# A four-layer graph network on one core: spreading the loop products over the first edge groups, and moving three weight loads

## The chip, the cores and the metric

The kernel runs on one core of one Trainium2 chip. The metric is the device time of one execution in microseconds (us), as the median of several runs. Engines are called as in the profile: PE (TensorE matmuls), PEld (TensorE weight loads), DVE (VectorE), ACT (ScalarE), POOL (GpSimd), SP (SyncE, which here only issues transfers).

## The reference

1024 nodes with 512 features, 17408 edges sorted by target node, all in float32. Four graph layers follow each other, each on the normalized, rectified features, each added back to `x`. The change lies in the last one, called block 3 here, which runs the following layer twice (8 relations, 4 bases):

```python
hb = jnp.einsum('nd,bdo->bno', h, basis)
coef = comp[etypes]
m = sum(coef[:, b, None] * hb[b][src] for b in range(4))
m = m * norm[:, None]
agg = jax.ops.segment_sum(m, dst, num_segments=n)
out = agg + bias + h @ loop_w
if apply_relu: out = relu(out)
```

The first layer (l = 0) has the relu, the second (l = 1) has not. `h @ loop_w` is the "loop product", `loop_w` the "loop weights".

## The kernel before, in words

The kernel first sums the edges' source rows per target and basis, and multiplies by the basis afterwards. Nodes come in 8 blocks of 128 (`n`), features in 4 chunks of 128 (`c`), edges in 68 groups of 256 (`g`; two tiles of 128, `k`). Only the arm `fast` runs here.

For each layer `l` of block 3, the loop at L1142 and following does this for each group `g`:

1. Two gathers on POOL (`gathered`, L1122 to L1129, `gather`, L289) fetch the 256 source rows of the *next* group from the table `htabs[l]` in HBM into tiles `m`. Eleven tiles exist for them (5 `m`, 4 `h`, 2 `hq`); a gather waits until the group that used its tile eleven gathers earlier is done.
2. DVE builds the weighted one-hot `wo` of the next group (L1135).
3. PE multiplies `m` and `wo` into `ps` (L1149, 16 matmul records per group).
4. At some groups (the table at L1151) PE also does the loop product of one node block `n`: `loop0(n)` for l = 0 (L1048, `dense`, matmuls on L251), and for l = 1 a transposition `turned5(n + 1)` (L241) and `loop1(n)` (L251, added by DVE at L1111; POOL adds the bias at L1112). The products of blocks 0 to 2 come ahead of group 0, those of 3 to 7 are in the table.
5. From group 11 on, when the sums of node block 0 are complete (`settled`), PE does two steps per group of the basis products (`products`, L1094, `po`), 16 steps per node block. Those left over come behind the last group.
6. DVE adds `ps` into `sums` (L1168).

A finished node block goes through `ready` (L1076 to L1087). For l = 0 it is added, rectified and stored by SP's queue to the table `htabs[1]` (L1082); the first gather of layer 1 needs all eight of these stores. For l = 1 it is stored to the output (L1087).

Weights: a pool of six half-tiles (512 KB each, tag `w`) holds the loop weights and bases 0 and 1 of a layer; basis 2 lies in `w_l0`, and basis 3 in the one tile `w4` (1 MB, L1104). All of these loads go by SP's queue. The loop weights of layer 1 are loaded in layer 0 behind group 8 (L1161, `loop_weights`: two halves and the bias row). Bases 0 to 2 of layer 1 and then basis 3 are loaded when the last products of layer 0 have released their tiles.

The order on each engine is not that of the text: a planner issues what it reckons ready first. `tc.issue_after(i)` queues what is traced in its body behind instruction `i` on `i`'s engine, without a wait for its end.

Of the kernel before, what the change touches and what calls it, by code (L numbers as in the profile page):

```python
# [21 lines left out]
P = 128  # L22
# [10 lines left out]
NBAS = 4  # L33
# [3 lines left out]
G = 2  # L37
# [12 lines left out]
def gnn_stack(ctx, tc, a, out, xtab, htabs, hidtab):  # L50
# [6 lines left out]
    nc = tc.nc  # L57
# [23 lines left out]
    src_i = const.tile([P, ET], I32, name="src_i")  # L81
# [6 lines left out]
    def half_w(name):  # L88
        return wpool.tile([P, 2, D], F32, tag="w", name=name, bufs=6)

    def load_half(w, ap, h):
        nc.sync.dma_start(w, ap.rearrange("(h c p) o -> h p c o", h=2, p=P)[h])
        return w
# [193 lines left out]
        return nc.vector.tensor_sub(lo, rest, mid).ins  # L287

    def gather(g, table, idx, t):  # L289
        nc.gpsimd.indirect_dma_start(  # L290
            out=g, out_offset=None, in_=table,
            in_offset=bass.IndirectOffsetOnAxis(ap=idx[:, t : t + 1], axis=0))

# [93 lines left out]
    def stack(fast):  # L387
# [529 lines left out]
        with tc.tile_pool(name=f"l2{fast}", bufs=1) as l2:  # L917
# [107 lines left out]
            def loop_weights(l):  # L1025
                return load_w(a[f"L3_gnn_loop{l}"], f"loop{l}{fast}"), bias_row(f"L3_gnn_bias{l}", f"l3_{l}{fast}")

            def bases(l):

                ws = [load_w(a[f"L3_gnn_basis{l}"][b], f"basis{l}_{b}{fast}") for b in range(2)]  # L1030
                return ws + [[load_half(w_l0[h], a[f"L3_gnn_basis{l}"][2], h) for h in range(2)]]
# [33 lines left out]
        with tc.tile_pool(name=f"l3{fast}", bufs=1, reuse_waits="tile") as l3:  # L1065

            sums = l3.tile([P, KC, NBAS, N], F32, name="sums")
            if fast:
# [5 lines left out]
                    nc.scalar.activation(sums[:, 1, 2:4], nil.to_broadcast([P, 2 * N]).rearrange("p (b d) -> p b d", b=2), AF.Copy)  # L1074
                nc.gpsimd.memset(sums[:, 3], 0.0)

            def ready(l, n, po):

                if l == 0:
                    nc.vector.tensor_add(hb[:, n, :], hb[:, n, :], po)  # L1080
                    nc.scalar.activation(hb[:, n, :], hb[:, n, :], AF.Relu)  # L1081
                    nc.sync.dma_start(htabs[1][n * P : (n + 1) * P, :], hb[:, n, :])  # L1082
                    if fast:
                        nc.gpsimd.memset(sums.rearrange("p c b d -> p (c b) d")[:, :, n * P : (n + 1) * P], 0.0)
                else:
                    nc.vector.tensor_add(x[:, n, :], x[:, n, :], po)
                    nc.sync.dma_start(out[n * P : (n + 1) * P, :], x[:, n, :])  # L1087
# [12 lines left out]
            for l in range(2):  # L1100
                if l == 1:
                    w3 = [loops[1][0]] + bases(l)
                w = l3.tile([P, KC, D], F32, tag="w4", name=f"basis{l}_{NBAS - 1}{fast}")
                nc.sync.dma_start(w, a[f"L3_gnn_basis{l}"][NBAS - 1].rearrange("(c p) o -> p c o", p=P))  # L1104
                w3.append(w)
                with tc.tile_pool(name=f"l3e{l}{fast}", bufs=3 if fast else 1, reuse_waits="tile") as l3e:
                    def turned5(n):
                        hT3[n] = transposed(hb[:, n, :], f"l3_1_{n}")

                    def loop1(n):  # L1110
                        nc.vector.tensor_add(x[:, n, :], x[:, n, :], dense(hT3[n], w3[0], f"pl_1_{n}"))  # L1111
                        nc.gpsimd.tensor_add(x[:, n, :], x[:, n, :], loops[1][1])  # L1112

                    if l == 1:
                        turned5(0)
                        for n in range(3 if fast else NB):
                            if n + 1 < NB:
                                turned5(n + 1)
                            loop1(n)

                    homes = 5 * [(l3e, "m", 5)] + 4 * [(work, "h", 4)] + 2 * [(small, "hq", 2)]

                    def gathered(g):
                        m = []
                        for k in range(G):
                            pool, tag, bufs = homes[(g * G + k) % len(homes)]
                            m.append(pool.tile([P, D], F32, tag=tag, name=f"m_{l}_{g}_{k}", bufs=bufs))
                            gather(m[k], htabs[l], src_i, g * G + k)
                        return m  # L1129

                    if fast:
                        def weighted(g):
                            wo = l3e.tile([P, G, NBAS, W], F32, tag="wo", name=f"wo_{l}_{g}")
                            ts = slice(g * G, (g + 1) * G)
                            nc.vector.tensor_mul(wo, ohw[:, ts, :].unsqueeze(2).to_broadcast([P, G, NBAS, W]),  # L1135
                                                 cw[:, l, ts, :].unsqueeze(3).to_broadcast([P, G, NBAS, W]))
                            return wo

                        todo = (step for n in range(NB) for step in products(l, n, w3))
                        given = 0  # L1140
                        nxt = gathered(0), weighted(0)
                        for g in range(NG):  # L1142
                            m, wo = nxt
                            if g + 1 < NG:
                                nxt = gathered(g + 1), weighted(g + 1)
                            ps = bank(f"ps_{l}_{g}")
                            for c in range(KC):
                                for k in range(G):
                                    nc.tensor.matmul(ps[:, c * P : (c + 1) * P], m[k][:, c * P : (c + 1) * P],  # L1149
                                                     wo[:, k].rearrange("p b w -> p (b w)"), start=(k == 0), stop=(k == G - 1))  # L1150
                            n = {0: 3, 1: 4, 2: 5, 4: 6, 6: 7}.get(g)  # L1151
                            if n is not None:
                                if l == 0:
                                    loop0(n)
                                else:
                                    if n + 1 < NB:
                                        turned5(n + 1)
                                    loop1(n)
                            if l == 0 and g == 8:

                                loops[1] = loop_weights(1)  # L1161
                            done = sum(settled(n) <= g for n in range(NB - 1))
                            for _ in range(2):
                                if given < done * NBAS * KC:
                                    next(todo)
                                    given += 1
                            part = sums.rearrange("p c b d -> p (c b) d")[:, :, bass.ds(base(g), W)]
                            nc.vector.tensor_add(part, part, ps.rearrange("p (i w) -> p i w", w=W))  # L1168
                        for _ in todo:
                            pass  # L1170
                    else:
                        for g in range(NG):
                            m = gathered(g)
                            for b in range(NBAS):
                                for j in range(2):
                                    wo = l3e.tile([P, G, 512], F32, tag="wo", name=f"wo_{l}_{g}_{b}_{j}")
                                    for k in range(G):
                                        t = g * G + k
                                        nc.vector.tensor_scalar(wo[:, k, :], iota[:, j * 512 : (j + 1) * 512], dst_f[:, t : t + 1],
                                                                cw[:, l, t, b : b + 1], op0=ALU.is_equal, op1=ALU.mult)  # L1180
                                    for c in range(KC):
                                        ps = bank(f"ps_{l}_{g}_{b}_{j}_{c}")
                                        for k in range(G):
                                            nc.tensor.matmul(ps, m[k][:, c * P : (c + 1) * P], wo[:, k, :],
                                                             start=(k == 0), stop=(k == G - 1))
                                        part = sums[:, c, b, j * 512 : (j + 1) * 512]
                                        if g == 0:
                                            nc.vector.tensor_copy(part, ps)
                                        else:
                                            nc.vector.tensor_add(part, part, ps)  # L1190
                        for n in range(NB):
                            for _ in products(l, n, w3):
                                pass
                        if l == 0:
                            loops[1] = loop_weights(1)
# [65 lines left out]
```

## Time and profile before

| | |
|---|---|
| runs | 1237.68, 1236.44, 1232.68 us; median 1236.44 |
| profiled execution | 1221.29 us |
| its span, first to last instruction | 1219.5 us |
| PE busy in the span | 1195.6 us (98%) |
| POOL busy in the span | 580.5 us (48%) |
| mean granted PE clock | 0.994 |

The profiled execution is 15 us shorter than the median of the runs; nothing in the profile says why. Block 3 starts with the first loop product at 688.8 us of the span; layer 0's groups start at 699.9 us, its last products end at 951.9 us, layer 1's groups start at 963.1 us and its last matmuls at 1212 us. A time such as 963.1 us is always counted from the start of the span. Matmul durations in the rows overlap; what one group costs PE is read from the starts of neighbours: 1.78 us for the `ps` of one group, 3.43 us for a loop product, 0.43 us for a transposition, 1.72 us for two steps of basis products.

### The profile page before, as it was taken

What the parts mean: (1) busy time and instruction counts of PE and PEld (TensorE: products, weight loads), DVE (VectorE), ACT (ScalarE), POOL (GpSimd) and SP (SyncE); (2) the same over time, 40 slices, a digit from 0 to 9 for tenths busy, and PEclk for the clock granted to TensorE, in tenths of its full rate; (3) what the DMA queues carried; (4) which work ended last, traced back from release to release, by engine and by line L of the source; (5) the groups of instructions that cost most, each with busy time, mean ns of one, the idle gap of its engine ahead of it and who ended that gap; (6) DMA issues with size and microseconds to landing.
All of it is one profiled execution on the core that took longest, in us unless ns stands there. A gap on an engine that the chain in (4) does not pass through costs nothing.

```text
span 1219.5 us, 17420 instructions
## 1 busy us (share of the span) xinstructions
PE 1195.6 (98%) x6322; PEld 795.8 (65%) x6322; DVE 661.8 (54%) x1244; ACT 295.0 (24%) x693; POOL 580.5 (48%) x641
## 2 busy tenths in 40 slices
PE   7999999999999999999999999999999999999998
PEld 3445557767777778644444567777776577777774
DVE  5888647786777775776774433333332153333331
ACT  4435364434444443432332400000000000000000
POOL 2011346686666663443121266566661586555540
PEclk9999999989999999999999999999999999999999
DMA  3331045545544442002002366555552666556540
GB/s 114 124 125 36 22 155 165 151 139 153 151 139 139 139 130 85 21 22 65 1 9 92 101 193 206 160 164 157 165 163 65 199 170 194 162 162 170 157 129 17
DMA packets 55166, 149.77 MB, mean 123 GB/s; under 512 B 8796, under 2 KB 10272, under 8 KB 55008
## 3 DMA queue, kind: packets, MB, share of 16 engines
q0 software_dynamic: 33360, 109.34, 31.3%
q1 hardware_dynamic: 21424, 38.71, 9.6%
q8 instruction: 52, 0.85, 0.3%
q10 hardware_dynamic: 288, 0.52, 0.1%
q14 instruction: 42, 0.34, 0.1%
HBM read 135.70 MB, written 12.85 MB: 122 GB/s over the span
## 4 chain that ended last, share of the span: by engine, by line
PE 89%; DVE 4%; issue 2%; DMA 2%; ACT 1%; POOL 1%; DVEq 0%; SPq 0%; ACTq 0%; POOLq 0%
PE ps L1149 19%; PE po L1094 18%; PE pg L885 14%; PE pu L275 10%; PE pw L819 10%; PE p L955 7%; PE pl L251 4%; PE pm L453 2%; PE po L803 1%; PE pz L251 1%; PE pt_l L241 1%; PE pc L532 1%; DVE cnt L545 1%; PE pup L689 1%; DMA w_mlp<-in_L_gnn_W_mlp_dram 1%
## 5 line engine op out<-in xcount | busy, mean ns | idle before, releaser
L290 POOL DMA_INDIRECT m<-htab_dram,src_i x272 | 261.2, 960 | 165.6 <-PE ps L1149 116.9
L1149 PEld LDWEIGHTS ps<-wo,m 128*128 128x128 f32 x2176 | 261.6, 192 | 57.3 <-issue 56.0
L1149 PE MATMUL ps<-wo,m 128*128 128x128 f32 x2176 | 262.2, 275 | 0.7 <-DMA m<-htab_dram,src_i 0.7
L885 PEld LDWEIGHTS pg<-yo,msg 128*128 128x128 f32 x1632 | 194.6, 193 | 35.9 <-issue 17.8
L885 PE MATMUL pg<-yo,msg 128*128 128x32 f32 (+1 forms) x1632 | 189.8, 274 | 2.7 <-DVE msg L841 1.5
L1168 DVE TENSOR_TENSOR sums<-sums,ps 128x512 f32 x136 | 93.7, 689 | 156.7 <-PE po L1094 133.8
L836 ACT ACTIVATE dot<-s,ea 128x128 f32<-128x128 f32 x408 | 130.0, 390 | 165.7 <-DVE msg L841 107.5
L290 POOL DMA_INDIRECT s<-xtab_dram,src_i x136 | 132.8, 976 | 36.4 <-issue 24.5
L819 PE MATMUL pw<-w_mlp,hq 128*128 128x512 f32 x272 | 135.1, 620 | 0.0
L1135 DVE TENSOR_TENSOR wo<-ohw,cwTrue 128x256 f32<-128x256 f16 x136 | 65.9, 487 | 103.5 <-PE ps L1149 103.5
L859 POOL TENSOR_TENSOR yo<-ohw,ea 128x160 f32<-128x160 f16 x136 | 63.1, 486 | 66.6 <-PE pg L885 66.5
L275 PE MATMUL pu<-parts,cnt 128*128 128x512 bf16 x384 | 84.8, 379 | 0.0
L837 DVE TENSOR_TENSOR msg<-pw,s 128x512 f32<-128x512 f32 x68 | 47.0, 692 | 47.3 <-PE pw L819 35.6
L819 PEld LDWEIGHTS pw<-w_mlp,hq 128*128 128x128 f32 x272 | 47.2, 193 | 34.0 <-issue 34.0
L275 PEld LDWEIGHTS <-cnt 128*128 128x128 f16 x384 | 37.6, 98 | 44.9 <-issue 2.3
L838 DVE TENSOR_TENSOR msg<-s,pw 128x768 f32<-128x768 f32 x68 | 64.2, 944 | 0.0
L1094 PE MATMUL po<-basis_0True,sums 128*128 128x512 f32 x128 | 60.8, 600 | 0.4
L1094 PE MATMUL po<-basis_3True,sums 128*128 128x512 f32 x128 | 59.8, 594 | 0.8 <-DVE sums L1168 0.8
L1081 ACT ACTIVATE stage<-stage 128x512 f32<-128x512 f32 x8 | 5.0, 630 | 226.9 <-DVE stage L1080 226.9
L1094 PE MATMUL po<-w_l,sums 128*128 128x512 f32 x128 | 59.9, 593 | 0.0
L1094 PE MATMUL po<-basis_1True,sums 128*128 128x512 f32 x128 | 59.9, 593 | 0.0
L888 DVE TENSOR_TENSOR acc<-acc,pg 128x256 f32 x68 | 28.7, 422 | 46.7 <-PE pg L885 46.7
(208 smaller groups left out, 1355.2 us busy)
## 6 DMA issues: line engine op xcount, KB each, us to landing
hq<-hidtab_dram SPq DMA_DIRECT2D x17, 256.0 KB, 2.9
m<-htab_dram,src_i POOLq DMA_INDIRECT x272, 3.6
hidtab_dram<-hid POOLq DMA_DIRECT2D x9, 256.0 KB, 2.3
s<-xtab_dram,src_i POOLq DMA_INDIRECT x136, 3.6
xtab_dram<-up SPq DMA_DIRECT2D x8, 256.0 KB, 2.0
b_1True<-in_L_gnn_W_dram SPq DMA_DIRECT2D x4, 512.0 KB, 5.0
w_l<-in_L_gnn_basis_dram SPq DMA_DIRECT2D x4, 512.0 KB, 4.3
basis_0True<-in_L_gnn_basis_dram SPq DMA_DIRECT2D x4, 512.0 KB, 4.0
```

The lines of the kernel that those rows point to most:

```text
L275: nc.tensor.matmul(pu, m[:, s, d * P : (d + 1) * P], z[:, s, :], start=(s == 0 and j == 0), stop=(s == NB - 1 and j == len(zs) - 1))
L290: nc.gpsimd.indirect_dma_start(out=g, out_offset=None, in_=table, in_offset=bass.IndirectOffsetOnAxis(ap=idx[:, t : t + 1], axis=0))
L819: nc.tensor.matmul(pw[:, k, :], hq[q][:, (t % 4) * P : (t % 4 + 1) * P], w_mlp4[:, t // 4 % 2, :], start=True, stop=True)
L836: nc.scalar.activation(dot[:, k, m, :], s1[:, k, m, :], AF.Copy, scale=ea[:, g * G + k, 1 + m : 2 + m])
L838: nc.vector.tensor_mul(msg[:, :, 2:5, :], s1, w[:, :, 2:3, :].to_broadcast([P, G, 3, MUL]))
L859: nc.gpsimd.tensor_mul(yo[:, k], ohw[:, t, :].unsqueeze(1).to_broadcast([P, NY, W]), ea[:, t, :].unsqueeze(2).to_broadcast([P, NY, W]))
L885: nc.tensor.matmul(ps[:, b : b + n, :], lhsT, rhs, start=(k == 0), stop=(k == G - 1))
L955: nc.tensor.matmul(p, lhs[:, c, :], rhs[:, c, :], start=(c == 0), stop=(c == 1))
L1094: nc.tensor.matmul(po, sums[:, c, b, n * P : (n + 1) * P], chunk(w3[1 + b], c), start=(b == 0 and c == 0), stop=(b == NBAS - 1 and c == KC ...
L1135: nc.vector.tensor_mul(wo, ohw[:, ts, :].unsqueeze(2).to_broadcast([P, G, NBAS, W]), cw[:, l, ts, :].unsqueeze(3).to_broadcast([P, G, NBAS ...
L1149: nc.tensor.matmul(ps[:, c * P : (c + 1) * P], m[k][:, c * P : (c + 1) * P], wo[:, k].rearrange("p b w -> p (b w)"), start=(k == 0), stop= ...
L1168: nc.vector.tensor_add(part, part, ps.rearrange("p (i w) -> p i w", w=W))
```

## The change

It has three parts.

**The table of loop products.** Block 3 stays with loop products 3 to 7 between groups, but 4 to 7 are put behind groups 2, 4, 6 and 9, not 1, 2, 4 and 6.

**The loop weights of layer 1.** They are no longer loaded behind group 8 of layer 0 in one go but in two halves, behind groups 24 and 32, each queued on SP behind the last store that has been traced.

**Basis 3 of layer 1.** Its 1 MB load leaves SP's queue. POOL issues it at group 2 of layer 1, behind the gathers of group 3. For layer 0 it stays where it was.

```diff
     def gather(g, table, idx, t):
-        nc.gpsimd.indirect_dma_start(
+        return nc.gpsimd.indirect_dma_start(
...
+            def loop_halves(l):
+
+                w = [half_w(f"loop{l}_{h}{fast}") for h in range(2)]
+                for h in range(2):
+                    load_half(w[h], a[f"L3_gnn_loop{l}"], h)
+                    if h == 0:
+                        loops[l] = w, bias_row(f"L3_gnn_bias{l}", f"l3_{l}{fast}")
+                    yield
...
+            stored, sent = [], []
...
-                    nc.sync.dma_start(htabs[1][n * P : (n + 1) * P, :], hb[:, n, :])
+                    stored.append(nc.sync.dma_start(htabs[1][n * P : (n + 1) * P, :], hb[:, n, :]).ins)
...
-                nc.sync.dma_start(w, a[f"L3_gnn_basis{l}"][NBAS - 1].rearrange("(c p) o -> p c o", p=P))
+                rows = a[f"L3_gnn_basis{l}"][NBAS - 1].rearrange("(c p) o -> p c o", p=P)
+                if l == 0 or not fast:
+                    nc.sync.dma_start(w, rows)
...
-                            gather(m[k], htabs[l], src_i, g * G + k)
+                            sent.append(gather(m[k], htabs[l], src_i, g * G + k).ins)
...
-                            n = {0: 3, 1: 4, 2: 5, 4: 6, 6: 7}.get(g)
+                            n = {0: 3, 2: 4, 4: 5, 6: 6, 9: 7}.get(g)
...
-                            if l == 0 and g == 8:
-
-                                loops[1] = loop_weights(1)
+                            if l == 0 and g in (24, 32):
+
+                                if g == 24:
+                                    halves = loop_halves(1)
+                                with tc.issue_after(stored[-1]):
+                                    next(halves)
+                            if l == 1 and g == 2:
+                                with tc.issue_after(sent[-1]):
+                                    nc.gpsimd.dma_start(w3[-1], rows)
```

## The prediction

> **What bounds the kernel now.** I read the page first: PE is busy for 1195.6 of 1219.5 us, and the chain that ended last is PE for 89%. A change of order can only win PE's idle time, so the second view was the busy time by stages, cut at block 3's borders.
>
> ```profile
> core 0: us, PE busy (x) PEld busy (x) DVE busy (x) ACT busy (x) POOL busy (x), PEclk, DMA share, GB/s
> ...
> 697.00:739.00 42.00, 42.00 (x242) 30.52 (x241) 17.30 (x31) 1.17 (x2) 28.52 (x30) 1.00 0.71 207
> 739.00:951.00 212.00, 211.62 (x1158) 149.64 (x1157) 68.87 (x121) 5.48 (x9) 113.75 (x113) 1.00 0.54 154
> 951.00:1005.00 54.00, 53.32 (x285) 36.92 (x284) 21.47 (x32) 4.15 (x7) 40.83 (x39) 1.00 0.59 170
> ```
>
> The first three figures are the stretch, its length and PE's busy time. Groups 0 to 11 of layer 0 (697 to 739), where the table and the loop weights change, hold no PE idle time at all; the same groups of layer 1 (951 to 1005) hold 54.00 - 53.32 = 0.68 us. Third, PE's waits from 690 us on, two in all:
>
> ```profile
> engine line waited for: us in total, times, longest us
> PE po L1094 <- DVE sums L1168: 0.8, 1, 0.8
> PE ps L1149 <- DMA m<-htab_dram,src_i: 0.7, 1, 0.7
> ```
>
> The 0.8 us is behind the last group of layer 1 (1198.11) and is not touched. The 0.7 us is the start of layer 1, and the chain of waits tells what it hangs on:
>
> ```profile
> 953.52 4.89 DMA htab_dram<-stage
> 960.55 3.59 DMA m<-htab_dram,src_i
> 964.18 1.83 PE ps L1149 x14
> ```
>
> The columns are start, duration, what. The last store of layer 0's result lands 4.89 us after its issue (958.41), the second gather is issued at 960.55, and PE gets its rows at 964.14, 0.68 us late. That is all of block 3's idle time which the change can reach.
>
> **Basis 3 leaves SP's queue.** Why does that store take 4.89 us? All eight stores of this line, and the transfer issued just ahead of it:
>
> ```profile
> L1082 SPq DMA_DIRECT2D htab_dram<-stage x8: 319/320/338, 766.4 to 953.5; - x8
> ...
> DMA to landing us min/median/max: 2.1/2.5/4.9
> ```
>
> ```profile
> q1 hardware_dynamic: 1029, 1.98, 59.2%
> issues: line engine op xcount, KB each, median us to landing
> basis_3True<-in_L_gnn_basis_dram SPq DMA_DIRECT2D x1, 1024.0 KB, 5.6
> htab_dram<-stage SPq DMA_DIRECT2D x1, 256.0 KB, 4.9
> ```
>
> Basis 3 is issued at 952.14 and lands 5.6 us later (957.7); the store behind it on the same queue lands 0.7 us after that. Its median is 2.5 us, with gathers running. Without basis 3 ahead I put it at 2.1 to 2.6 us: landing at 955.6 to 956.1 in place of 958.4. The first gather followed the landing by 959.27 - 958.41 = 0.86 us, so it could start at 956.5 to 957.0; POOL's bias add (956.35, 1.26 us) may come first, so I take 957.8. The second gather is issued 1.28 us later and lands 3.6 us after that, at 962.7. PE is through its two first matmuls at 963.50. So the whole 0.68 us goes, with 0.8 us to spare; it stays whole as long as the store lands within 4.2 us. No more than that can go, since PE works from 951 to 963.1 without a gap. The range of this term is 0 to -0.68; I take **-0.68 us**, since every store without basis 3 ahead lay near 2.5.
>
> **Basis 3 enters POOL's queue.** The trace has no 1 MB load on POOL. The nearest row is a 256 KB store by POOL (L458) at 0.54 us of POOL's time; the gathers of this stage cost 0.96 us each and follow each other every 1.26 us. So the issue costs between 0.54 and 4 x 0.54 = 2.2 us, and I take 1.1, near the gather. Behind it wait the gathers of group 4. In layer 1 as changed, POOL runs gathers 0 to 3 from 957.8, one add (1.43 with its gap), gathers 4 to 7, and issues basis 3 at about 969.4; with one more add, the gathers of group 4 start at 971.9 and 973.2 and land 3.6 us later, 976.8. PE as changed: group 0 from 963.1, the loop product (0.43 + 3.43) to 968.8, groups 1 and 2 to 972.3, a loop product to 976.2, group 3 to 978.0, and then group 4. That is 1.2 us to spare, so **0 us**. The other end: the 1 MB goes first and the gathers land the longest basis 3 landing (6.7 us) later, at 983.5; then PE waits 5.5 us. The value at 0 is the nearer, since gathers that shared the engines with a 1 MB load at 728 to 735 were 1.4 us later at most (5.0 us in place of 3.6). Basis 3 itself is needed at group 17, some 45 us after its issue, against a landing of 5.6 to 6.7.
>
> [...]
>
> **The table of loop products.** The same five blocks, 5 x 3.43 us per layer, are moved and none is added. What changes is how early rows are needed. Layer 0 as changed: group 0 at 699.94, product to 705.16, groups 1 and 2 from 705.16 and 706.95. Group 2's second gather is issued at 701.45 and lands 3.7 us later, 705.15, so 1.8 us remain. Groups 3, 4 are needed at 712.17 and 713.95, their gathers land at 707.6 and 710.1. For groups 5 to 11 the gathers are held by their tiles, not by POOL's pace, and land 5 us or more ahead. In layer 1, group 2 is needed at 970.55 and its second gather (965.6) lands at 969.6 if it takes 4.0 us. So **0 us** in both layers. The cover is this lead; without any lead a bare pair of groups costs 2.52 (two gathers) - 1.78 = 0.74 us per group. The bare stretch of five groups (7 to 11) is already run without a wait, 8.93 us for 80 records, so breaking it up wins nothing in this execution.
>
> **The loop weights in halves.** The same two loads and the bias row, three issues of about 0.3 to 0.4 us on SP, go from 728 us to behind the stores of blocks 0 and 1 (766.4 and some 28 us later). SP then has nothing but stores about 28 us apart, and waits on PE or ACT for the rest; queued behind the loads is the next such store. The tiles are free since loop product 7, and the weights are used from 951 on. In the new place the gathers' lead is five groups of 3.5 us, against 1.4 us of delay: **0 us**. At the old place the gathers' delay (4.2 to 5.0 us in place of 3.6) was covered too, so nothing comes back.
>
> **Sum.** -0.68 + 0 + 0 + 0 = -0.7 us. On the profiled execution: 1221.29 - 0.7 = 1220.6 us. The runs' median is 15 us above the profiled execution, with no cause in the profile; taken as common to both kernels, 1236.4 - 0.7 = **1235.7 us**.
>
> **Rivals.**
>
> *Nothing comes back* (1236.4 us). The store's 4.89 us would be due to bases 0 to 2, issued at 940 to 949 on the same queue, and stay over 4.2 us. For it: they are 3 MB. Against: the transfer rate falls to 16 and 0 GB/s between 952.5 and 953.0, so they had ended before the store was issued at 953.52.
>
> *The gathers queue behind basis 3* (slower; 1238.4 us, at most 1241.3). Place: group 4 of layer 1. It decides from where group 4's second gather lands more than 4.8 us after its issue (978.0 - 973.2). For it: the store behind basis 3 on SP. The price is 0 to 5.5 us, less the 0.68 won; I put it at about half, +2.0. Against it: the 1.2 us to spare, and one loop product behind group 4 in which the lead recovers.
>
> *The cover is worth more in the timed runs* (1229.0 us). If what makes them 15 us longer lies partly in late gathers, the bare five groups of each layer cost up to 10 x 0.74 = 7.4 us, which the new table would cover. For it: the 15 us are unexplained, and these are the groups in which POOL's pace is slower than PE's. Against: the profile has not one such wait in groups 7 to 11 of either layer, and leads of 5 us.
>
> *The change doesn't do what it says*: the planner places POOL's load elsewhere, or loop products float ahead of the first groups as two transpositions do at 933.73. If it floats behind the gathers of later groups, the time is that of the sum.
>
> **How the numbers follow.** The runs before lie within 0.4% of each other, so 0.5% (6.2 us) is about what a measurement here can tell from no change. Chances: forecast, with the planner's variants, 0.52; nothing comes back 0.17; gathers behind basis 3 0.19; worth more in the timed runs 0.12. Of the slower rival only its tail, its last 5 us together with a spread of the runs, passes 0.5%: 0.07, and 0.01 more for the spread alone. So faster 0.12, same 0.80, slower 0.08. The forecast's own range is 1235.7 with the runs' spread of 2.5 us to each side, 1233 to 1238.5. The range reaches to within 1 us of the fast rival and to the end of the slow one's price: 1230 to 1241.5.
>
> **What would show it.** In the profile after: the last store of layer 0 lands in 2.1 to 2.6 us; the first gather of layer 1 starts at 956.5 to 958; PE's wait on `m` at the start of layer 1 is gone, and PE's idle time from 951 to 1005 is under 0.1 us; basis 3 is issued by POOL at about 969 for about 1.1 us. A wait of PE for `m` at group 4 would show the slower rival. A median more than 6 us from 1236.4 with both stretches as I have them would prove that the runs spend time where the profile shows none.

## The result, and the profile after

The changed kernel takes 1228.07 us (median of 21 runs, 1225.34 to 1236.63). The kernel before took 1233.94 us beside it (21 runs, 1230.01 to 1240.34). The ratio is 0.9957, with a 95% interval of 0.9944 to 0.9971: the change is 5.3 us faster (3.6 to 6.9). The forecast was 1235.7 us with a range of 1230 to 1241.5.

One thing has to be known to read the numbers below. The same kernel has two levels of time, and one of them lasts for as long as a set of runs on a chip does. The kernel before took 1221.57, 1221.57 and 1221.60 us on three occasions (the *low level*), and 1233.94, 1234.02, 1233.61, 1234.24 and 1230.62 us on five others (the *high level*). One chip showed both, on different occasions. The profiled execution that was shown of before (1221.29 us) is of the low level, and the runs shown with it are of the high one: that is 12 of the 15 us that the prediction could not explain. The other 3 are the spread of the three runs shown, whose median (1236.44) lies above that of all 21 (1233.94). The profile after is of the high level.

Four views of the changed kernel, in the order of the prediction. First the busy time by stages (stretch, length, PE's busy time):

```profile
core 0: us, PE busy (x) PEld busy (x) DVE busy (x) ACT busy (x) POOL busy (x), PEclk, DMA share, GB/s
697.00:739.00 42.00, 39.37 (x206) 27.14 (x205) 15.23 (x27) 1.24 (x2) 26.96 (x29) 0.96 0.62 175
739.00:951.00 212.00, 211.73 (x1182) 151.64 (x1181) 70.61 (x124) 5.48 (x9) 115.72 (x114) 1.00 0.53 155
951.00:1005.00 54.00, 54.00 (x263) 35.22 (x262) 17.35 (x28) 4.14 (x7) 37.85 (x37) 1.00 0.61 187
```

The start of layer 1 (951 to 1005) has no PE idle time left, where before had 0.68 us. But the start of layer 0, which held none at all, now holds 2.63 us, at a clock of 0.96. PE's waits from 690 us on say the same:

```profile
engine line waited for: us in total, times, longest us
PE po L1105 <- DVE sums L1187: 1.9, 2, 1.1
PE pl L251 <- issue: 1.8, 1, 1.8
PE ps L1162 <- issue: 0.8, 2, 0.4
```

The wait on `m` is gone. New are PE's stops with "issue", time in which PE waited for nothing that the profile shows, and a second wait for DVE's sums (1.1 us, at 1023 us). The chain of waits at the start of layer 1 is PE alone; store and gathers no longer stand in it:

```profile
964.98 3.44 PE pl L251 x8
968.42 1.78 PE ps L1162 x16
```

How soon the store lands cannot be read from this trace, because it has lost records. The page's list of transfers gives a median time to landing for the gathers in every profile of the low level (3.5 or 3.6 us), and none here:

```profile
m<-htab_dram,src_i POOLq DMA_INDIRECT x272
```

That is general. Each of the eleven traces of the low level holds 13250 to 13254 semaphore updates and 8541 or 8542 landings of transfers; each of the nine traces of the high level holds 10995 to 11327 and 6581 to 6918.

### The profile page after: what moved, and what is told of

It reads as the page before. It is cut to its first block, busy times and chain, and to the rows that moved or that the text cites. A ratio compares the mean times of both kernels' runs of the same rounds, so it can differ in the third digit from the quotient of the medians.

```text
span 1225.3 us, 17400 instructions
## 1 busy us (share of the span) xinstructions
PE 1197.7 (98%) x6306; PEld 797.1 (65%) x6322; DVE 658.7 (54%) x1244; ACT 295.0 (24%) x693; POOL 581.8 (47%) x642
## 3 DMA queue, kind: packets, MB, share of 16 engines
q0 software_dynamic: 33632, 110.39, 31.1%
## 4 chain that ended last, share of the span: by engine, by line
PE 91%; DVE 3%; issue 2%; ACT 1%; DMA 1%; POOL 1%; DVEq 0%; SPq 0%; ACTq 0%
PE ps L1162 19%; PE po L1105 18%; PE pg L885 14%; PE pu L275 10%; PE pw L819 10%; PE p L955 7%; PE pl L251 5%; PE pm L453 3%; PE po L803 1%; PE pz L251 1%; PE pt_l L241 1%; PE pc L532 1%; DVE cnt L545 1%; PE pup L689 1%; DMA w_mlp<-in_L_gnn_W_mlp_dram 1%
```

## The experiments

### The parts, one at a time

The question going in was where the 5.3 us come from; the expectations set three theories, T1 to T3, against each other, each a wait of PE at another place. Four kernels ran on one chip, which turned out to be at the low level (before: 1221.57 us). First the kernel before once more, then each part of the change's diff alone: the table; the loop weights in halves behind groups 24 and 32; basis 3 by POOL.

> The kernel before, unchanged, for a second trace of it. The one trace shown before took 1221.29 us, while the 21 timed executions took 1230 to 1240. Theory T1 (the loop weights of layer 1, loaded behind group 8, collide with the bare groups 7 to 11): a trace of usual length (1230 us or more) shows PE waiting between 725 and 745 us of the span, 3 us or more in all, gaps and a lowered clock together. Theory T2 (the bare groups have too little lead, whatever is loaded): PE waits for m in groups 7 to 11 of both layers, about 3 us in each. Theory T3 (the store behind basis 3 lands later than in the one trace): PE waits 3 us or more at the start of layer 1. Null (time is lost elsewhere in the kernel, and the change only shifts what comes later): no wait of PE over 1 us in block 3. Ratio to before 1.000 in all.

1221.99 us, ratio 1.0007 (0.9989 to 1.0025); PE waits 0.9 us at the start of layer 1.

```diff
-                            n = {0: 3, 1: 4, 2: 5, 4: 6, 6: 7}.get(g)
+                            n = {0: 3, 2: 4, 4: 5, 6: 6, 9: 7}.get(g)
```

> Only the table of loop products is changed ({0: 3, 2: 4, 4: 5, 6: 6, 9: 7}); loop weights and basis 3 as before. T1: the cover lies over part of the load's stretch, so about half of the change's gain, 0.998 (-2 to -3 us). T2: nearly the whole gain, 0.996. T3 and null: 1.000.

1221.64 us, 1.0010 (0.9996 to 1.0024); the wait at layer 1 stays, 0.73 us.

```diff
...
-                            if l == 0 and g == 8:
-
-                                loops[1] = loop_weights(1)
+                            if l == 0 and g in (24, 32):
+                                if g == 24:
+                                    halves = loop_halves(1)
+                                with tc.issue_after(stored[-1]):
+                                    next(halves)
```

> Only the loop weights of layer 1 go in halves behind groups 24 and 32 of layer 0; table and basis 3 as before. T1: nearly the whole gain, 0.996 (-4 to -5 us). T2 and T3: 1.000. Null: 1.000, or a shift of either sign below 0.3%.

1221.68 us, 0.9999 (0.9982 to 1.0015); the wait stays, 0.6 us.

```diff
...
-                nc.sync.dma_start(w, a[f"L3_gnn_basis{l}"][NBAS - 1].rearrange("(c p) o -> p c o", p=P))
+                rows = a[f"L3_gnn_basis{l}"][NBAS - 1].rearrange("(c p) o -> p c o", p=P)
+                if l == 0 or not fast:
+                    nc.sync.dma_start(w, rows)
...
+                            if l == 1 and g == 2:
+                                with tc.issue_after(sent[-1]):
+                                    nc.gpsimd.dma_start(w3[-1], rows)
```

> Only basis 3 of layer 1 goes by POOL's queue behind the gathers of group 3; table and loop weights as before. T3: nearly the whole gain, 0.996 (-4 to -5 us). T1 and T2: the 0.7 us of the recorded prediction, 0.9995. The table of before puts groups 1 and 2 behind a loop product each, so group 4's rows are needed at about 982 us and no wait for them can appear.

1221.22 us, 1.0006 (0.9987 to 1.0025); the wait is gone. So the wait of 0.7 us belongs to basis 3, as predicted, and none of the parts moves the time by more than a measurement can tell. None of the 5.3 us is here, though: this chip does not have the 12 us that before spent in the first comparison, so T1 to T3 are not decided by these runs.

### Before and after again, and the cover in front of layer 1

> The kernel before, unchanged, for a third trace. In the first comparison it took 1234 us, in the second 1222 us, on another chip, and there none of the three parts alone moved the time. Theory T4 (on the chip of the first comparison PE runs at half its clock for about four windows of 3.4 us where block 3's groups begin, as the trace of the changed kernel shows it from 700 to 714 us, and the kernel before pays this at both layers' starts): a trace near 1234 us shows results of PE coming late at about 700 and at about 964 us, some 5 us each. If before takes about 1222 us here, nothing of that is in its trace. Rival: the 12 us lie all over the kernel.

1220.68 us, 1.0004 (0.9986 to 1.0021), the low level again, so theory T4 is not put to its test. What it reads off the first trace after is not there as written: that trace has the full clock from 700 to 708 us and a mean of 0.81 from 708 to 716, and in finer steps a clock of 0.50 from 712.93 to 716.33: one stretch of 3.4 us at half clock and not four.

> The changed kernel. T4: where before takes about 1222 us, the recorded prediction holds, 0.9994 (-0.7 us), within 0.998 to 1.001; where it takes about 1234 us, 0.9957 again. Rival (the change saves 5 us on any chip and the three parts do so only together): 0.996 in both cases.

1221.26 us, 0.9996 (0.9976 to 1.0016). At the low level the change measures 0.5 us, near the forecast's 0.7 and not to be told from nothing. This trace has kept its records, so the steps for basis 3 can be read. First the eight stores of layer 0's result:

```profile
L1093 SPq DMA_DIRECT2D htab_dram<-stage x8: 319/323/338, 769.7 to 956.8; - x8
...
DMA to landing us min/median/max: 2.0/2.5/2.7
```

The longest landing is 2.7 us; in before it was 4.9. Then POOL, with start and duration in front:

```profile
959.81 0.96 POOL L290 DMA_INDIRECT m<-htab_dram,src_i  x1 [2.53 <-DMA htab_dram<-stage]
960.79 1.27 POOL L1125 TENSOR_TENSOR x<-x,row_l_1True 128x512 f32<-128x512 f32 x1
962.22 0.97 POOL L290 DMA_INDIRECT m<-htab_dram,src_i  x1 [0.16 <-issue]
...
971.90 0.83 POOL L1180 DMA_DIRECT2D basis_3True<-in_L_gnn_basis_dram  x1
972.74 1.31 POOL L1125 TENSOR_TENSOR x<-x,row_l_1True 128x512 f32<-128x512 f32 x1
974.20 1.00 POOL L290 DMA_INDIRECT m<-htab_dram,src_i  x1 [0.16 <-issue]
975.51 0.95 POOL L290 DMA_INDIRECT m<-htab_dram,src_i  x1 [0.30 <-DMA m<-htab_dram,src_i]
```

The first gather starts 2.98 us after the last store's issue (956.83); in before it was 5.75. Basis 3 costs POOL 0.83 us. The two gathers behind it are those of group 4, and this is their row, with the load's own from the list of transfers:

```profile
DMA to landing us min/median/max: 5.7/6.0/6.4
```

```profile
basis_3True<-in_L_gnn_basis_dram POOLq DMA_DIRECT2D x1, 1024.0 KB, 8.0
```

They take 6.4 and 5.7 us where gathers take 3.5. Basis 3 lands at 971.90 + 8.0 = 979.9, the gathers at 980.6 and 981.2, and PE needs them at 981.47, the start of group 4. So they landed behind the load, on the queue that it shares with them (the page's q0 moves 110.39 MB in place of 109.34), as the rival said, and fell just inside the cover: 0.3 us were to spare, not 1.2.

The next kernel takes the cover away: one loop product fewer lies ahead of group 0 of layer 1.

```diff
-                        for n in range(3 if fast else NB):
+                        for n in range(2 if fast else NB):
...
+                            if l == 1 and g == 0:
+                                turned5(3)
+                                loop1(2)
```

> The kernel before with one loop product fewer ahead of layer 1's group 0: blocks 0 and 1 come ahead, block 2 follows group 0. PE's wait there should grow from 0.7 us by one loop product and one transposition, 3.87 us, to about 4.5 us. Work and loads are the same. If a wait is worth no more than its length: 1.0032 (+3.9 us). T4, by which a wait at a layer's start also takes the clock down: the granted clock falls to half behind it, for one window of 3.4 us or more, and the time grows by 5.5 us or more, 1.0045 to 1.008.

1227.02 us, 1.0045 (1.0024 to 1.0066): 5.5 us more (2.9 to 8.1) for a wait of 3.3 us, 2.6 us longer than that of before at this place. PE's waits from 690 us on, the gather that it waits for in the chain, and the clock (the third figure from the right is PE's granted clock, before DMA share and GB/s) behind it:

```profile
PE ps L1149 <- DMA m<-htab_dram,src_i: 3.3, 1, 3.3
```

```profile
956.89 4.78 DMA htab_dram<-stage
...
962.52 3.42 DMA m<-htab_dram,src_i
```

```profile
965.00:970.00 5.00, 3.92 (x15) 2.92 (x16) 0.00 (x0) 0.58 (x1) 4.16 (x5) 0.66 0.60 175
```

A mean of 0.66 over 5 us is 3.4 us at half the clock, which costs an estimated 1.7 us, half of it, on top of the wait. 2.6 + 1.7 = 4.3 us is what this trace explains; the runs cannot tell it from 5.5. In before, whose wait at this place is 0.7 us, the clock from 965 to 970 is 1.00.

The kernel before a fourth time, the same cut of the cover in the changed kernel, and before with all five loop products 3 to 7 behind group 0 of each layer, so that no group from 1 to 11 has one:

> The kernel before, unchanged, once more, in search of the 12 us that separate the first comparison (1234 us) from the later ones (1222 us, where PE's waits in block 3 are the 0.7 to 0.9 us of the recorded prediction). T4: if before takes some 1234 us here, its trace has results of PE late by 4 us or more at about 700 us, and again at about 964 us. Rival: the 12 us lie all over the kernel. If it takes 1222 us, nothing follows.

1224.51 us (8 runs, 1218.84 to 1226.48), 1.0011 (0.9990 to 1.0033); the low level.

> The changed kernel with one loop product fewer ahead of layer 1's group 0 (it follows group 0), the same edit that cost the kernel before 5.5 us. In the changed kernel the first gather of layer 1 was issued 2.98 us behind the store, before it was 5.75 us. Theory T5 (the moved basis 3 is worth nearly 3 us of lead, of which the cover leaves 0.7 to be seen): the wait is 3.3 - 2.8 = 0.5 to 1.5 us and the time against before 1.0005 to 1.002, so that the change is worth some 4 us where the cover is short. Rival (the lead is lost again, to POOL's bias add between the first two gathers): as without the change, 1.0045.

1223.08 us, 1.0026 (1.0004 to 1.0047). PE waits twice on `m`, 1.5 and 0.5 us, in place of 3.3 us. The store lands in 2.04 us, and what holds the second gather is now POOL's bias add (1.27 us), which the prediction had named as the next in line. So the moved basis 3 leaves less of the lead than T5 expected (waits of 0.5 to 1.5 us, 1.0005 to 1.002), and more than its rival did; the time alone does not tell the two apart, since 1.0045 lies within the interval.

```diff
-                            n = {0: 3, 1: 4, 2: 5, 4: 6, 6: 7}.get(g)
-                            if n is not None:
+                            for n in range(3, NB) if g == 0 else ():
```

> The kernel before with all five loop products 3 to 7 behind group 0 of each layer, so that groups 1 to 11 run bare. By the recorded prediction a bare group costs at most 0.74 us and only without lead: POOL needs 2.52 us for two gathers, eleven tiles hold 5.5 groups, and the five products give POOL 17 us; groups 1 to 11 need 22 gathers, 27.7 us, against 17.2 + 11 x 1.78 = 36.8 us of PE: no wait, 1.000. Theory T2 (bare groups cost time): a wait in groups 7 to 11, up to 0.74 x 11 x 2 = 16 us, 1.003 to 1.013.

1222.52 us, 1.0011 (0.9993 to 1.0028), with waits of 1.3 us on `m` in all of block 3, the longest 0.8. Eleven bare groups in a row cost next to nothing at the low level.

### The high level, with half as much traffic again

The kernel before and the changed one, each with one more store per group in groups 0 to 11 of both layers, on one chip. It was the chip of the last three kernels, now at the high level (before: 1234.02 us).

```diff
...
+                            if g < 12:
+                                row = (l * 12 + g) * P
+                                nc.sync.dma_start(spare[row : row + P, :], m[0])
```

> Before, with one more transfer per group in groups 0 to 11 of both layers: one of the group's two gathered tiles is stored to a spare table (24 x 256 KB in all, half as much again as the gathers move there). The output is unchanged. It asks whether slow transfers in these groups can be what the first comparison lost. Theory A (the cover was worth more in the first comparison because gathers landed late): the gathers land well over 5 us after their issue, PE waits on m in the bare groups 5 to 11, and the time rises by 3 to 12 us. Rival B (late gathers stay covered): gathers up to 5 us, no wait of PE on m past group 2, the time within 1.5 us of before.

1233.18 us, 1.0010 (0.9993 to 1.0027): no more than before takes there.

> The changed kernel with the same 24 stores. Theory A: it loses at least 3 us less than before does with them, which would be the size of the 5.3 us of the first comparison. Rival B: the two lose the same within 1.5 us, and slow transfers in these groups are not what told the two kernels apart there. If both lose much and by the same amount, the cover is too small to tell, and A falls as well.

1227.96 us, 0.9963 (0.9944 to 0.9982): the gain of the first comparison within the intervals. So the stores (in before's order 254 GB/s from 697 to 739 us, without them 207) change neither kernel's time, and theory A falls: slow transfers are not what the table covers. How late the gathers landed cannot be read in full, since the traces of this level have lost records. Of one gather of group 4 in the changed kernel it can, and there the cover was gone:

```profile
981.38 6.39 DMA m<-htab_dram,src_i
...
987.81 1.64 PEld L1162 LDWEIGHTS ps<-wo,m 128*128 128x128 f32 x14 [0.30 <-DMA m<-htab_dram,src_i]
```

The first line is of the chain, the second of PE's weight loads in order of time. The gather was issued behind basis 3, and groups 3 and 4 take 0.4 us longer than at the low level.

But now there is a trace of before's order at the high level. Its chain of waits at the end of the bare groups 7 to 11 of layer 0, first in before at the low level and then in this run:

```profile
729.78 8.93 PE ps L1149 x80
738.71 1.72 PE po L1094 x4
740.43 1.78 PE ps L1149 x16
```

```profile
732.63 8.93 PE ps L1149 x80
741.57 2.28 issue
743.85 3.15 PE po L1094 x4
747.00 2.29 PE ps L1149 x16
```

Behind the 80 matmul records PE stands still for 2.28 us, its next four matmul records take 3.15 us in place of 1.72, and the next group 2.29 in place of 1.78: 4.2 us are lost. At the same place of layer 1:

```profile
1002.57 8.93 PE ps L1149 x80
1011.50 0.86 issue
1012.36 1.96 PE po L1094 x4
1014.32 1.78 PE ps L1149 x16
1016.10 2.53 issue
1018.63 1.98 PE po L1094 x4
```

0.86 + 0.24 + 2.53 + 0.26 = 3.9 us. A third stop lies at group 2 of layer 0, where 16 records take 3.47 us in place of 1.78. Together that is 9.8 of the 12 us between the levels. Theory T4 had two places, 700 and 964 us, at half clock. The stops lie at three others, and only at the second is the clock lowered (a mean of 0.91 from 734 to 752 us, in this run; 1.00 from 700 to 721 and from 1003 to 1022, where the other two lie). In the changed kernel the picture is another one. This is its chain at the start of layer 0, at the high level (the last run below); at the low level group 1 starts at 708.51 and group 3 at 715.51, 7.0 us later, without a stop:

```profile
705.12 3.49 PE ps L1162 x30
...
709.33 0.70 issue
710.04 0.68 PE pl L251
710.72 1.40 issue
712.12 4.88 PE pl L251 x7
717.00 3.57 PE ps L1162 x32
```

From 705.12 to 717.00 it takes 11.9 us: the stop in front is now 4.9 us long, and those behind the bare groups are gone or small.

### Which part of the change moves the stops

Three kernels on another chip, at the high level (before: 1233.61 us): the table alone again; the change without its table; and before with 144 short copies on ACT, which is busy for 1.17 of the 42 us from 697 to 739 in before.

> Before with the new table of loop products and nothing else of the change, in the hope of a chip that runs before at 1234 us, as the first comparison and the last one did. Theory C: on such a chip PE stands still for about 4 us at the end of the bare groups 7 to 11 of each layer (741.6 and 1011 to 1020 us in the last trace of before with stores), and the table alone breaks these groups up and wins 4 to 8 us, ratio 0.993 to 0.997. Rival D: the 5 us come from the loads that were moved (no 1 MB of loop weights at 728 us, no basis 3 on SP's queue), and the table alone stays within 1.5 us of before. On a chip that runs before at 1222 us both expect no difference.

1230.83 us, 0.9974 (0.9952 to 0.9997).

> The change without its table: loop weights in halves and basis 3 by POOL, the loop products where they were before. Theory C: within 1.5 us of before on a chip that runs before at 1234 us, with both stops of PE at the end of the bare groups. Rival D: all of the 5 us, ratio about 0.996, with the stops gone. On a chip that runs before at 1222 us: within 1.5 us of before for both.

1232.17 us, 0.9998 (0.9974 to 1.0021). So the table alone is faster, if only just, and the rest alone is not told from nothing: theory C, though its 4 to 8 us were too much (3.2, with 0.4 to 5.9 as the interval). Rival D falls, since its 0.996 lies outside the interval of the change without the table, and the stops are still there. The two runs themselves are not told apart, for their intervals overlap; that the table is the part which acts rests on the stops as well. T1 falls with the same run, as the loads in halves are in it. T2 and T3 wanted waits of 3 us and more for gathers; in before's order at this level PE waits for `m` 0.5 or 0.6 us in all. PE's waits from 690 us on, without the table and with it alone:

```profile
PE po L1105 <- issue: 5.0, 2, 2.5
PE ps L1162 <- issue: 1.0, 1, 1.0
```

```profile
PE ps L1149 <- issue: 2.6, 3, 1.8
PE po L1094 <- issue: 1.2, 1, 1.2
PE pl L251 <- issue: 1.2, 1, 1.2
...
PE ps L1149 <- DMA m<-htab_dram,src_i: 0.7, 1, 0.7
```

Without the table both long stops are in front of `po`, behind the bare groups; with it they are mostly in front of `ps` and `pl`, at group 2 of layer 0 and the product behind it. The wait on `m` is there only where basis 3 is still on SP's queue.

```diff
+                            if g < 12:
+                                tick = small.tile([P, 1], F32, tag="tick", name=f"tick_{l}_{g}")
+                                for j in range(6):
+                                    nc.scalar.copy(tick, wo[:, 0, 0, j : j + 1])
```

> Before with six copies of a single column by ACT in each of groups 0 to 11 of both layers: 144 instructions on an engine that has no work there, in a tile that nobody reads; the output is unchanged. Theory E (where before takes 1234 us, the recording of the run holds the engines up where many short instructions and transfers end at once, as the many lost records there suggest): more records there cost more, and the time rises by 2 us or over on such a chip. Rival F (the stops of PE come from PE's own load, by its clock or its supply): ACT's copies change nothing, within 1 us. On a chip that runs before at 1222 us both expect no difference.

1232.48 us, 0.9996 (0.9975 to 1.0017), with the three stops of before. Theory E falls in this form: 144 more short instructions on ACT cost nothing that the runs can tell.

### A third table

If the order alone sets the stops, the first three groups of before and the short bare stretches of the change should be better than both:

```diff
-                            n = {0: 3, 2: 4, 4: 5, 6: 6, 9: 7}.get(g)
+                            n = {0: 3, 1: 4, 2: 5, 5: 6, 8: 7}.get(g)
```

> The changed kernel with a third table: loop products 3 to 7 behind groups 0, 1, 2, 5 and 8, so that the first three groups have a product behind each, as before, and no more than three bare groups follow each other, as in the change. Theory C, from the stops read off the last traces: where before takes 1234 us, the stop at group 2 of layer 0 is 1.4 to 2.2 us (before's order) and not 5 to 6 (the change's), and those at groups 9 to 13 of both layers are 0 to 1.6 us each, so 2 to 5 us in all against 9.3 to 10 in before and 6.6 to 8.6 in the change: 1225 to 1228 us, ratio 0.993 to 0.996, 1 to 4 us better than the change. Rival G (the stops belong to the places, not to the order, and what is taken from one comes at the next): the ratio of the change, 0.996 to 0.997, or worse. Where before takes 1222 us: 0.998 to 1.001 for both.

1225.85 us (6 runs), 0.9935 (0.9910 to 0.9959), before at 1234.24 us. That is what theory C expected, but the interval meets that of the change. So the two ran side by side, on a chip with before at 1230.62 us:

> The third table once more, on the same chip as the change itself. Theory C: where before takes 1234 us, 0.992 to 0.996 and 1 to 4 us under the change; stops of 1.4 us at group 2 of layer 0 and 2 to 4 us in layer 1. Rival G: as the change, within 1 us of it.

1226.58 us, 0.9970 (0.9952 to 0.9987).

> The changed kernel beside the third table. Theory C: 0.995 to 0.997 where before takes 1234 us, with a stop of 5 to 6 us at group 2 of layer 0 and one of 1 to 2 us in layer 1. Rival G: as the third table, within 1 us of it. Where before takes 1222 us, both within 1 us of before.

1225.67 us, 0.9963 (0.9947 to 0.9979). The third table is not better than the change in the runs (0.9 us behind it): what theory C expected of the time is not borne out here, and rival G, within 1 us, fits. The traces show the stops shifted once more, as C said at group 2 of layer 0 (1.4 and 1.5 us), while those of layer 1 grew. The table gives PE's lost time in us at the high level, as the growth of its delay against a trace of the low level at points where as much work is done:

| kernel | group 2, layer 0 | groups 9 to 13, layer 0 | groups 11 to 16, layer 1 | sum |
|---|---|---|---|---|
| before's order, with stores | 1.7 | 4.2 | 3.9 | 9.8 |
| before's order, change without table | 1.4 | 3.1 | 4.4 | 8.9 |
| before's order, with ACT's copies | 2.1 | 4.5 | 4.3 | 10.9 |
| change (first comparison) | 5.1 | 0 | 1.5 | 6.6 |
| change, with stores | 5.2 | 0 | 1.1 | 6.3 |
| table alone | 6.2 | 0 | 1.6 | 7.8 |
| change, beside the third table | 4.9 | 0 | 1.3 | 6.2 |
| third table | 1.4 | 0.6 | 2.9 | 4.9 |
| third table, beside the change | 1.5 | 0.7 | 3.0 | 5.2 |

The 0.4 us of the gather behind basis 3 are left out of the row with stores. By these sums the third table should win 1 to 2 us on the change, which is within what the runs can tell.

## Why the prediction was wrong

**What bounds the kernel, and what basis 3 holds up: right.** PE's wait on `m` at the start of layer 1 went with basis 3 (present with the table or the halves alone, gone with basis 3 alone), its idle time from 951 to 1005 is nil, and the eight stores land in 2.0 to 2.7 us, where 2.1 to 2.6 were foreseen (first gather 2.98 us after the last one's issue). The term of 0.68 us agrees with 0.5 us at the low level, which no run there can tell from nothing: the wait's end is shown by the traces, its worth by no time.

**Basis 3 in POOL's queue: 0, as forecast, but by less than thought.** The issue took 0.83 us in place of the 1.1 taken. The gathers of group 4 did go behind the load and landed 2.2 to 2.9 us later than usual. The cover held with 0.3 us to spare, since POOL had issued them about 1 us earlier against group 0 than reckoned. With the extra stores it did not hold, and 0.4 us were lost.

**The halves: 0, right** at both levels as far as the runs tell (0.9999 alone; 0.9998 together with basis 3 at the high level).

**The table: 0 at the low level, right; wrong at the high one.** "Breaking it up wins nothing in this execution" was true of the execution that the profile showed, and only of it.

**The step that failed** is the last one of the sum: the 15 us of the runs over the profiled execution, "taken as common to both kernels". They were not. Before loses 9 to 11 us at the high level in three stops of PE, two of them right behind the five bare groups; the changed table loses 6 to 8. That is about 3 us, the table's 3.2 us in the runs; with basis 3's wait (0.5 to 0.7 us in the traces of this level that have it) it makes nearly 4 of the 4.6 to 5.3 us that the change won in its three comparisons at the high level. At the low level the forecast for the profiled execution, -0.7 us, stands (0.5 measured). The prediction's last paragraph had named the sign of the failure: a median over 6 us away (it was 8.3) means that the runs spend time where the profile of before shows none.

**The rivals.** "The cover is worth more in the timed runs" gave 1229.0 us, and named the right edit and one of the right places (groups 7 to 11). That its number lies within 1 us of the result is luck: its mechanism, late gathers, is not the one. With half as much traffic again the kernels keep their times, and in those traces PE waits for `m` 0.6 us in before's order and loses 0.4 us in the changed one. "The gathers queue behind basis 3" was right in that they land behind it, and wrong in its price of 2 us: nothing at the low level, 0.4 us with the extra stores. "Nothing comes back" fell with the store's landing. That the change might not do what it says did not come: POOL issues basis 3 behind the gathers of group 3, and the loop products lie where the table puts them.

**What stays open** is what stops PE. The stops come where groups run at full rate, in the first groups of layer 0 and behind bare ones in both layers, but only at the high level. A half-clock window is recorded at some of them (708 to 716 in the first profile after, mean clock 0.81, below) and not at others (1.00 from 700 to 730 and from 1003 to 1024 in the first run of the third table). Every trace of that level has lost records, and every timed run is recorded as well (each has its span and clock), so no run here shows whether the recording is the cause, or a kernel without it would lose the time too. ACT's extra instructions speak against a recorder shared by all engines, not against one of PE's own. Whether PE's instructions come late is not tested either; all that the pages show is that the row of the instruction queue q8 is the same at both levels (52 packets, 0.85 MB, 0.3%).

## What to carry to other kernels

Check that the profiled execution belongs to the runs: if its time lies outside them by more than their spread, find out what differs before a sum is made on it, since the missing time may depend on the very order that is being changed. A stretch without a wait in one profile is not proved to be free in the runs; run the edit alone, at the same level as the comparison. And when a load is moved to the queue of the gathers, count how late the gathers behind it land (here 2.2 and 2.9 us), not only the issue (0.83 us).

## What the hardware showed that was not expected

The two levels themselves: 1221.6 us and 1231 to 1234 us for one kernel, on one and the same chip on different occasions, with records lost on every occasion of the upper one.

DVE took a result of PE 6.9 us after PE's last record of it began. At the high level DVE's adds of groups 1 and 2 start at 713.92 and 714.86 in the changed kernel, although PE's records have group 1 begin at 705.35 (the first line is the add of the product ahead of it):

```profile
709.47 0.69 DVE L1057 TENSOR_TENSOR stage<-pl,row_l_0True 128x512 f32<-128x512 f32 x1 [4.48 <-PE ps L1162]
713.92 0.69 DVE L1187 TENSOR_TENSOR sums<-sums,ps 128x512 f32 x1 [3.76 <-remote]
...
714.86 0.68 DVE L1187 TENSOR_TENSOR sums<-sums,ps 128x512 f32 x1
```

At the low level the add of group 1 starts 0.3 us behind the start of its group's last matmul record (710.49 against 710.18); here it is 6.9 us behind (713.92 against 707.02; both record times are the group's start and 15 records of 0.111 us). So PE's busy time from 705.00 to 708.50 looks full (3.50 us of 3.50) while what hangs on it falls behind, and DVE's waits (4.48 and 3.76 us in these rows) show it. Whether the matmuls themselves are late or only the signal of their end, these rows do not tell; so the place of a stop in PE's records need not be where it began. The clock there, with the same stretch of before at the low level second:

```profile
708.00:716.00 8.00, 5.37 (x16) 2.61 (x15) 2.65 (x5) 0.00 (x0) 4.34 (x5) 0.81 0.52 148
```

```profile
708.00:716.00 8.00, 8.00 (x34) 4.65 (x33) 2.12 (x5) 0.00 (x0) 6.17 (x7) 1.00 0.73 208
```

And one wait of PE cost more than its length: behind the one of 3.3 us (before with less cover) the mean clock was 0.66 from 965 to 970, 3.4 us at half the clock, which adds an estimated 1.7 us. Behind the waits of 1.5 and 0.5 us in the changed kernel with less cover PE is not slowed: 14 matmul records of `ps` take 1.83 us, as in before, and the loop product its 3.44.
